# An attention and density kernel whose PSUM jobs no longer wait for the other bank's readers, with new caps on two engines' unused time

## The chip, the cores and the metric

The kernel runs on one core of a Trainium2 chip. The metric is the device time of one launch in microseconds; before the change the median of three runs is 4970.23 us (4967.25 to 4970.26). The profile is one further execution of the same program. TensorE (PE) does the matmuls and transposes, ScalarE (ACT) the activations, VectorE (DVE) reductions and elementwise work, GpSimd (POOL) some elementwise work, and SyncE (SP) issues the loads and stores.

## The reference

The input `x` is 8 images of 192 channels and 64 x 64 pixels, fp32. Two layers follow each other, each on a group norm of its input (32 groups) and each added to it.

```python
# layer 0: x = x + attention(_gn(x))
q = prelu(conv1x1(x, w1, b1), a1)            # 24 channels
k = prelu(conv1x1(x, w2, b2), a2)            # 24 channels
v = prelu(conv1x1(x, wa, ba), aa)            # 192 channels
score = jax.nn.softmax(jnp.einsum('bnc,bcm->bnm', q, k), axis=2)   # 4096 x 4096 per image
out = jnp.einsum('bnm,bmc->bnc', score, v)
# layer 1: x = x + density(_gn(x)); the chain below for x - 0.5 (lower) and for x + 0.5 (upper)
for i in range(4):                            # widths 1, 3, 3, 3, 1, weights per channel
    logits = jnp.einsum('cij,cjn->cin', softplus(ms[i]), logits) + bs[i]
    if i < 3:
        logits = logits + jnp.tanh(fs[i]) * jnp.tanh(logits)
sign = -jnp.sign(lower + upper)
likelihood = jnp.maximum(jnp.abs(sigmoid(sign * upper) - sigmoid(sign * lower)), 1e-6)
```

## The kernel before, in words

**Steps.** An image has 4096 queries in 8 blocks of 512, and a block is worked off in 16 steps of 256 keys, so an image takes 128 steps and the whole launch 1024. In step `t` the program writes, in this order: the score matmuls of the next step (`scores`, L738), the matmuls for a row maximum that will be needed 22 steps later (`max_products`, L669) and its reduce on VectorE (`max_reduce`, L677), the exponential on ScalarE (L742), and the eight products of the exponentials with the values (`attend`, L753), which accumulate in PSUM over a block's 16 steps. Then `work_off` adds everything else that falls into this step. The scores have one tile of two PSUM banks, the maxima have one, and two more such tiles (`turns`, named b0 and b1) take turns: one accumulates the block, the other is free for jobs. Each engine executes its own instructions in the order in which the program wrote them.

**Jobs.** A job is a piece of PSUM work that isn't part of the step: keys, queries and values of the next image (`keys`, L573; `queries`, L602; `values`, L630), the transposes that put the row maxima into the queries (`max_end`: `turn` L705, `add` L710), a block's output transposes (`finish`: `turn` L786, `residual` L795), the two small matmuls of a norm (`norm_end`: `mean` L420, `second`, `variance` L433, `third` L438) and the products that fold a norm into the weights (`weights`: `products`, `offsets`). `start_job` gives a job one bank or both of the free tile, and notes until which step it holds them. A job's matmuls come first; in the steps after that ScalarE or VectorE reads the result. Waits are derived from the order of accesses to a tile. A job in one bank therefore also waits for what earlier instructions read from the other bank of that tile.

**Density.** Layer 1 of an image is cut into 12 units (`Unit`, 128 x 1024 elements), and a unit into three lists of instructions, one for each of VectorE, ScalarE and TensorE. An image's units join the queue `units` when its second norm is known, which is some steps into the next image, and are worked off during that image's steps. VectorE's part is `scalar_tensor_tensor` (L995), ScalarE's are tanh (L963, L978) and scaled copies (L972, L988). In each step `density_step` adds a rate to each engine's credit. For VectorE the rate is found anew each step: the work left, spread over the steps up to a deadline of 10 steps past the next image, and a small addition. `Unit.step` then writes instructions while the credit is above zero, each costing about 1.2 us of it, and only those whose inputs were written in an earlier step. A job's cost is taken off as well. The credit is capped: VectorE's at twice the rate, ScalarE's at its own rate, which is 2.9 in the steps. Up to three units are worked at a time, the oldest first, and only the oldest is removed when its VectorE list is empty. The end of a pair of units (lower and upper) is `ending`: a few instructions on VectorE, ScalarE or GpSimd and a store.

**Ends of the launch.** Ahead of the steps stands a head that norms the first image and makes its keys, queries and values. After the last step comes a tail in which the last image's norm is found and its 12 units are worked off. There, 11 of the 12 units take their first mixing layer to TensorE (`product`, L936, in all four tiles; `gate1`, L954, follows on VectorE). In the tail the rate is 4.15 and the end of a pair stays on VectorE and ScalarE (`alone`).

Of the kernel before, what the change touches and what calls it, by code (L numbers as in the profile page):

```python
# [17 lines left out]
def kernel(  # L18
# [45 lines left out]
    F = 512  # L64
# [260 lines left out]


    homes = []

    scratch = []
    for k, cols in (("a", F), ("b", 2 * C)):  # L330
# [3 lines left out]
            pair.append(u)  # L334
        scratch.append(pair)
    ready = [0, 0]

    def start_job(t):
        p = t % STEPS
        for n, (rank, make, hold, banks, cols) in enumerate(jobs):  # L340
            if stream[0] and (p < 3 or p + max(hold, 1) >= STEPS):
                continue
            rooms = [(pm, g) for pm, g in homes if sum(k <= t for k in g) >= banks]
            if not rooms:
                if rank < 2:
                    return
                continue
            k = [i for i in (1, 0) if ready[i] <= t and scratch[i][0].shape[1] >= cols]
            if cols and not k:
                continue  # L350
            del jobs[n]
            pm, guest = min(rooms, key=lambda r: max(r[1]))
            at_ = [i for i in range(2) if guest[i] <= t]
            for i in at_[:banks]:
                guest[i] = t + hold + 1
            if cols:
                ready[k[0]] = t + 2
            parts = make(pm if banks == 2 else pm[:, at_[0], :], scratch[k[0]] if cols else None)
            for i, fn, cost, act, pe in parts:
                at(t + i, fn, cost, act, pe)  # L360
            return
# [47 lines left out]
    def norm_end(key, n, t, then=None):  # L409
# [7 lines left out]

        def mean():
            pm = cell["pm"]
            nc.tensor.matmul(pm[:, 0:2], lhsT=gavg, rhs=cell["mv"], start=True, stop=True)  # L420

        def second():
            mv, pm = cell["mv"], cell["pm"]
            res = cell["res"] = small.tile([128, 2], F32, tag="nrm", bufs=4, name=f"nrm_{nm}")
            nc.vector.tensor_copy(res, pm[:, 0:2])
            dv = cell["dv"] = small.tile([128, 2], F32, tag="dv", name=f"dv_{nm}")
            nc.vector.tensor_tensor(dv[:, 0:1], mv[:, 0:1], res[:, 0:1], ALU.subtract)
            nc.vector.tensor_tensor(dv[:, 0:1], dv[:, 0:1], dv[:, 0:1], ALU.mult)
            nc.vector.tensor_copy(dv[:, 1:2], dv[:, 0:1])

        def variance():
            pm = cell["pm"]
            nc.tensor.matmul(pm[:, 2:4], lhsT=gavg, rhs=cell["dv"], start=True, stop=True)  # L433

        def third():
            res, pm = cell["res"], cell["pm"]
            ve = cell["ve"] = small.tile([128, 1], F32, tag="ve", name=f"ve_{nm}")
            nc.vector.tensor_tensor(ve, res[:, 1:2], pm[:, 2:3], ALU.add)  # L438
# [36 lines left out]

        def make(pm, _):
            cell["pm"] = pm
            return [
                (0, mean, 0.0, 0.0, 0.4), (1, second, 0.8, 0.0, 0.0),
                (2, variance, 0.0, 0.0, 0.4), (3, third, 0.4, 0.0, 0.0),  # L480
            ]
# [7 lines left out]
    def weights(b, then):  # L489
        res = norms[b, 0]  # L490
        cell = {}

        def scale():
            for k, src, n in (("q", w1r, 2), ("k", w2r, 1), ("v", wa_sb, 1)):
                d = wf[k, b] = fold.tile(
                    [128, 3, src.shape[2]], F32, tag=f"w{k}", bufs=n, name=f"w{k}_{b}"
                )
                nc.scalar.activation(d, src, AF.Copy, scale=res[:, 1:2])
            mb = cell["mb"] = fold.tile([128, 128], F32, tag="mb", name=f"mb_{b}")
            nc.vector.tensor_copy(mb, res[:, 0:1].to_broadcast([128, 128]))  # L500

        def products():
            pf = cell["pf"]
            p = slice(0, R)
            for g in range(3):
                nc.tensor.matmul(
                    pf[:, 0:2], lhsT=wf["q", b][p, g, :], rhs=res[p, 0:2],
                    start=g == 0, stop=g == 2,
                )
            for g in range(3):  # L510
                nc.tensor.matmul(
                    pf[:, 2:4], lhsT=wf["k", b][:, g, :], rhs=res[:, 0:2],
                    start=g == 0, stop=g == 2,
                )
            for g in range(3):
                nc.tensor.matmul(
                    pf[:, 4 : 4 + C], lhsT=cell["mb"][p], rhs=wf["v", b][p, g, :],
                    start=g == 0, stop=g == 2,
                )

        def offsets():
            pf = cell["pf"]
            for k, src, at_, n in (("bq", bq, 0, 2), ("bk", bk, 2, 1)):
                d = wf[k, b] = fold.tile([128, 2], F32, tag=k, bufs=n, name=f"{k}_{b}")
                nc.vector.tensor_tensor(
                    d[:, 0:1], src[:, 0:1], pf[:, at_ : at_ + 1], ALU.subtract
                )
                nc.vector.tensor_scalar(d[:, 1:2], d[:, 0:1], -1.0, None, ALU.mult)
            d = wf["ba", b] = fold.tile([128, C], F32, tag="ba", name=f"ba_{b}")
            nc.vector.tensor_tensor(d, ba_row, pf[:, 4 : 4 + C], ALU.subtract)  # L530
            then()

        at(now[0] + 1, scale, 0.3, 2.0)
        def make(pf, _):
            cell["pf"] = pf
            return [(0, products, 0.0, 0.0, 2.0), (1, offsets, 1.0, 0.0, 0.0)]

        at(now[0] + 3, lambda: job(make, 1))
# [10 lines left out]

    made = set()  # L550

    def prelu(name, dst, src, bias, nslope, u):


        def first():
            for i, sign in enumerate((1.0, -1.0)):
                b_ = bias[:, i : i + 1] if bias is not None else 0.0
                nc.scalar.activation(u[i], src, AF.Relu, bias=b_, scale=sign)

        def last():  # L560
            nc.vector.scalar_tensor_tensor(dst, u[1], nslope, u[0], ALU.mult, ALU.add)
            made.add(name)

        return first, last

    def keys(b, d, what, done):
        t = xi[what, b, d]

        def make(pk, u):
            if b not in kt:  # L570
                kt[b] = kpool.tile([128, N // 4], F32, tag="k", name=f"k_{b}")
            for g in range(3):
                nc.tensor.matmul(  # L573
                    pk[:, 0:P], lhsT=wf["k", b][:, g, :], rhs=t[:, g, :],
                    start=g == 0, stop=g == 2,
                )
# [4 lines left out]
            first, last = prelu(  # L581
                ("k", b, d), kt[b][p, at_ : at_ + P], pk[p, 0:P], wf["bk", b][p], nslope[p, 1:2],
                [x[p, 0:P] for x in u],
            )
            return [
                (0, lambda: None, 0.0, 0.0, 1.3), (1, first, 0.0, 0.9, 0.0),
# [104 lines left out]
    def max_end(b, n):  # L691
# [10 lines left out]
        def turn():  # L702
            pt = cell["pt"]
            for t in range(4):
                nc.tensor.transpose(pt[:, t * 128 : (t + 1) * 128], nm[:, t, :], ident)  # L705

        def add():
            u = (n % 2) * 256
            q = qt[b, n // 2][:, :, u : u + 256]
            nc.vector.tensor_tensor(  # L710
                q, q, cell["pt"].rearrange("p (s t) -> p s t", s=2), ALU.add
            )
            made.add(("max", b, n))

        def make(pt, _):
            cell["pt"] = pt
            return [(0, turn, 0.0, 0.0, 0.8), (1, add, 0.7, 0.0, 0.0)]

        at(now[0], collect, 0.4)
# [140 lines left out]
    class Unit:  # L860
# [146 lines left out]
        def more(self, k):  # L1007
# [258 lines left out]
    for d in range(NP):  # L1266
# [1 line left out]
            norm_stat((0, 0), 2 * d + k, flat(xi["first", 0, d], k))  # L1268
    spread()
    negatives()  # L1270
    others = [
        ps_sc.tile([128, 2, F], F32, tag="sc", name="sc_head"),
        ps_mx.tile([128, 2, F], F32, tag="mx", name="mx_head"),
    ]
    homes.extend((t, [0, 0]) for t in turns + others)

    def go_on():
# [103 lines left out]
```

## Time and profile before

| what | value |
|---|---|
| median of three runs | 4970.23 us |
| the profiled execution's own time | 4970.59 us |
| its span, first to last instruction | 4968.6 us |
| PE busy in the span | 4785.8 us (96%) |
| DVE busy | 4301.2 us (87%) |
| ACT busy | 3202.4 us (64%) |
| POOL busy | 513.9 us (10%) |
| mean granted TensorE clock | 0.984 |

The profile's page shares out the span; a group line gives a source line, an engine, the tiles written and read, the count, the busy time and the mean of one, and what ended the idle time before them. A line of the waits view says who waited for whom: total us, times, longest. In a timeline row the start and the duration come first; brackets at its end tell how long the engine had been idle and what released it. PEld is the loading of weights, which overlaps the matmuls. A matmul in fp32 is recorded as two, so a step's eight `attend` products show as 16 rows. The steps fill the span from 93 to 4616 us, the head lies before, the tail behind.

### The profile page before, as it was taken

How to read it: one execution, taken by the hardware profiler on the slowest of the kernel's cores; microseconds unless marked ns; L12 is line 12 of the kernel's file. 1: busy time of each engine (PE TensorE's matmuls, PEld its weight loads, DVE VectorE, ACT ScalarE, POOL GpSimd, SP SyncE). 2: the span in 40 equal slices, each digit the busy share in tenths (PEclk: the TensorE clock that was granted, in tenths of full speed). 3: DMA queues.
4: the chain of work that ended last, by engine and by line, in shares of the span. 5: the costliest groups of instructions: out<-in, count | busy, mean ns of one | idle time of the engine just before them, and what ended most of it. 6: DMA issues, size and time to landing. Idle time of an engine off the chain costs nothing.

```text
span 4968.6 us, 69863 instructions
## 1 busy us (share of the span) xinstructions
PE 4785.8 (96%) x29152; PEld 3525.8 (71%) x29152; DVE 4301.2 (87%) x4442; ACT 3202.4 (64%) x3709; POOL 513.9 (10%) x506
## 2 busy tenths in 40 slices
PE   7999999999999999999999999999999999999596
PEld 5777777777777777777777777777777777777242
DVE  5433359999899989999899999999899999999888
ACT  2333346776667767777667766776677766776665
POOL 0000001111012110112011210110101110110000
PEclk9999999999999999999999999999999999999798
DMA  2000020011200111010200111011111111000000
GB/s 57 24 23 17 14 52 15 21 24 35 49 18 18 41 37 34 22 34 24 60 15 21 41 27 40 18 35 31 31 34 28 27 29 24 11 20 7 9 11 15
DMA packets 111953, 135.48 MB, mean 27 GB/s; under 512 B 14739, under 2 KB 93077, under 8 KB 111637
## 3 DMA queue, kind: packets, MB, share of 16 engines
q1 hardware_dynamic: 110432, 130.65, 10.9%
q8 instruction: 228, 3.74, 0.3%
q14 instruction: 89, 0.72, 0.1%
q10 hardware_dynamic: 1204, 0.37, 0.0%
HBM read 105.82 MB, written 25.17 MB: 26 GB/s over the span
## 4 chain that ended last, share of the span: by engine, by line
PE 73%; DVE 22%; ACT 3%; issue 1%; POOL 1%; DMA 0%; POOLq 0%; ACTq 0%; SPq 0%; DVEq 0%
PE b L753 43%; PE sc L738 17%; DVE d L995 14%; DVE rm L677 5%; PE b L630 3%; PE b L936 2%; PE b L602 1%; PE b L573 1%; PE mx L669 1%; PE sc_tail L936 1%; PE mx_tail L936 1%; PE b L786 1%; ACT d L988 1%; ACT d L963 1%; PE b L705 1%
## 5 line engine op out<-in xcount | busy, mean ns | idle before, releaser
L753 PEld LDWEIGHTS b<-v,e 128*128 128x128 f32 x16384 | 2668.4, 191 | 781.5 <-issue 781.5
L753 PE MATMUL b<-v,e 128*128 128x193 f32 x16384 | 2972.7, 335 | 0.0
L742 ACT ACTIVATE e<-sc 128x1024 f32<-128x1024 f32 x1024 | 1046.3, 1022 | 1422.6 <-PE mx L669 1373.3
L677 DVE TENSOR_REDUCE rm<-mx 128x1 f32<-128x1024 f32 x1002 | 1222.0, 1220 | 522.2 <-PE mx L669 518.5
L738 PE MATMUL sc<-q,k 25*128 25x512 f32 x4096 | 1159.7, 642 | 5.5 <-ACT e L742 5.2
L669 PE MATMUL mx<-k,q 24*128 24x512 f32 x4008 | 1135.6, 643 | 13.1 <-DVE rm L677 13.0
L995 DVE SCALAR_TENSOR_TENSOR d<-d,wsp,d 128x1024 f32<-128x1024 f32 x768 | 985.8, 1284 | 47.5 <-ACT d L988 35.4
L995 DVE SCALAR_TENSOR_TENSOR d<-d,lc,d 128x1024 f32<-128x1024 f32 x765 | 968.4, 1279 | 16.3 <-ACT d L972 3.3
L995 DVE SCALAR_TENSOR_TENSOR d<-d,tf,d 128x1024 f32<-128x1024 f32 x543 | 681.5, 1280 | 4.0 <-ACT d L978 3.9
L978 ACT ACTIVATE d<-d 128x1024 f32<-128x1024 f32 x543 | 570.1, 1055 | 70.8 <-DVE d L995 69.3
L738 PEld LDWEIGHTS sc<-q,k 25*128 25x128 f32 x4096 | 306.8, 183 | 238.6 <-issue 198.8
L1077 POOL MEMSET pause<- 128x1 f32 x240 | 23.7, 99 | 4007.4 <-DVE d L995 4007.4
L988 ACT ACTIVATE d<-d,cb,wsp 128x1024 f32<-128x1024 f32 x351 | 433.1, 1235 | 6.6 <-DVE d L995 5.3
L963 ACT ACTIVATE d<-xc,bn,wn 128x1024 f32<-128x1024 f32 x288 | 353.2, 1233 | 7.8 <-DVE bn L467 7.0
L669 PEld LDWEIGHTS mx<-k,q 24*128 24x128 f32 x4008 | 300.2, 183 | 40.1 <-DVE rm L677 39.9
L972 ACT ACTIVATE d<-xc,bn,wn 128x1024 f32<-128x1024 f32 x255 | 314.6, 1234 | 0.1
L1124 POOL TENSOR_TENSOR d<-d,d 128x512 f32<-128x512 f32 x80 | 167.9, 2098 | 0.1
L1112 POOL TENSOR_TENSOR d<-d,d 128x512 f32<-128x512 f32 x80 | 166.3, 2079 | 7.7 <-DVE d L995 7.1
L1132 POOL TENSOR_TENSOR d<-d,d 128x512 f32<-128x512 f32 x80 | 159.3, 1992 | 2.1 <-POOL pause L1077 0.3
L630 PE MATMUL b<-wv,xi 64*128 64x192 f32 x1344 | 139.5, 340 | 0.0
L630 PEld LDWEIGHTS b<-wv,xi 64*128 64x128 f32 x1344 | 106.5, 186 | 25.4 <-issue 23.8
L1116 ACT ACTIVATE d<-d 128x512 f32<-128x512 f32 x160 | 91.8, 623 | 32.1 <-POOL d L1112 26.0
(171 smaller groups left out, 2372.3 us busy)
## 6 DMA issues: line engine op xcount, KB each, us to landing
xi<-in_x_dram SPq DMA_DIRECT2D x392, 192.0 KB, 3.6
xc<-in_x_dram SPq DMA_DIRECT2D x64, 384.0 KB, 8.2
out_dram<-xc SPq DMA_DIRECT2D x96, 256.0 KB, 3.2
d<-in_x_dram SPq DMA_DIRECT2D x16, 192.0 KB, 4.3
d<-in_wat_dram ACTq DMA_DIRECT2D x2, 144.0 KB
cb<-in_den_b_dram SPq DMA_DIRECT2D x6, 2.2 KB, 2.1
ff<-in_den_f_dram SPq DMA_DIRECT2D x6, 2.2 KB, 2.1
bq<-in_b_dram ACTq DMA_DIRECT2D x4, 0.1 KB
```

The costliest lines, as they stand in the source:

```text
L630: nc.tensor.matmul(pv[:, s, 0:C], lhsT=t[p, g, k * 128 : k * 128 + 128] if g < 3 else one_row[p], rhs=wf["v", b][p, g, :] if g < 3 else wf ...
L669: nc.tensor.matmul(sc[:, s, :], lhsT=tile_of(qt[b, n // 2], n, j)[r], rhs=kt[b][r, u : u + F], start=True, stop=True,)
L677: nc.vector.tensor_reduce(out=rowmax[b, n][:, j, k : k + 1], in_=sc, axis=AX.XY, op=ALU.max)
L738: nc.tensor.matmul(sc[:, s, :], lhsT=kt[b][r, k : k + 128], rhs=qt[b, n // 2][r, :, u : u + 256], start=True, stop=True,)
L742: return lambda: nc.scalar.activation(e, sc, AF.Exp)
L753: nc.tensor.matmul(a[:, j, 0 : C + 1], lhsT=e[:, s, j * 128 : j * 128 + 128], rhs=v[:, s, p % 4, :], start=p == 0 and s == 0 and j % 2 == ...
L936: nc.tensor.matmul(out[:, h, :], lhsT=diag[g][:, 3 * i + n - 1 if n else 9 + i, :], rhs=src[:, h * F : h * F + F], start=n == 0, stop=n == 3,)
L963: nc.scalar.activation(self.buf[k], self.src(), AF.Tanh, bias=bn[:, s, g, 0, i : i + 1], scale=wn[:, g, 0, i : i + 1],)
L972: nc.scalar.activation(self.buf[k], self.src(), AF.Identity, bias=bn[:, s, g, 1, i : i + 1], scale=wn[:, g, 1, i : i + 1],)
L978: nc.scalar.activation(self.buf[k], self.buf["l", k[1], k[2]], AF.Tanh)
L988: nc.scalar.activation(self.buf[k], self.buf["l", n - 1, 0], AF.Identity, bias=offset, scale=wsp[:, g, w : w + 1],)
L995: nc.vector.scalar_tensor_tensor(dst, src, factor, dst, ALU.mult, ALU.add)
```

## The change

It has four parts. First, a job's matmuls (`write`) and the readers of its result (`read`) are registered so that a matmul in one bank is no longer ordered behind readers of the other bank of the same tile; this covers the norm's, the weights', the keys' and the maxima's jobs, those that hold one bank. Second, with two units left, the one with more VectorE work left goes first, a unit is removed as soon as its list is empty, and a pair's ending waits until both of its units are done. Third, in the steps the cap on the credits of VectorE and ScalarE becomes the rate plus 1.3; in the tail both caps stay as they were. Fourth, the deadline of an image's density is 15 steps past the next image instead of 10. The two tiles of the head are allocated earlier, so that they can be named.

```diff
+    def spotted():
+        n, i = spot[0]
+        def write(inst):
+            tc.declare_no_dep(inst.ins, group=f"turn{n}{1 - i}", reason="reads the other bank")
+        def read(inst):
+            tc.add_to_no_dep_group(f"turn{n}{i}", inst.ins)
+        return write, read
...
+            spot[0] = next(n for n, k in enumerate(turns + others) if k is pm), at_[0]
             parts = make(pm if banks == 2 else pm[:, at_[0], :], scratch[k[0]] if cols else None)
...
-            nc.tensor.matmul(pm[:, 0:2], lhsT=gavg, rhs=cell["mv"], start=True, stop=True)
+            cell["write"](
+                nc.tensor.matmul(pm[:, 0:2], lhsT=gavg, rhs=cell["mv"], start=True, stop=True)
+            )
...
-            nc.vector.tensor_tensor(ve, res[:, 1:2], pm[:, 2:3], ALU.add)
+            cell["read"](nc.vector.tensor_tensor(ve, res[:, 1:2], pm[:, 2:3], ALU.add))
...
         def make(pk, u):
...
+            write, read = spotted()
             for g in range(3):
-                nc.tensor.matmul(
+                write(nc.tensor.matmul(
                     pk[:, 0:P], lhsT=wf["k", b][:, g, :], rhs=t[:, g, :],
                     start=g == 0, stop=g == 2,
-                )
+                ))
...
-                nc.tensor.transpose(pt[:, t * 128 : (t + 1) * 128], nm[:, t, :], ident)
+                cell["write"](
+                    nc.tensor.transpose(pt[:, t * 128 : (t + 1) * 128], nm[:, t, :], ident)
+                )
...
                 b, c, g, s = self.key
-                if s == 1:
+                if not any(u.key == (b, c, g, 1 - s) and u.todo["DVE"] for u in units):
                     ending(b, c, g)
...
-            rate = left * COST["DVE"] / max(1, (units[0].key[0] + 2) * IMG + 10 - t) + OTHER
-        credit["DVE"] = min(credit["DVE"] + rate, 2 * rate)
+            rate = left * COST["DVE"] / max(1, (units[0].key[0] + 2) * IMG + 15 - t) + OTHER
         act = ACT_RATE if t < last else rate
-        credit["ACT"] = min(credit["ACT"] + act, act)
+
+        for eng, most in (("DVE", rate), ("ACT", act)):
+            more = (rate if eng == "DVE" else 0.0) if t >= last else 1.3
+            credit[eng] = min(credit[eng] + most, most + more)
         credit["PE"] = min(credit["PE"] + rate, rate)
         for eng in ("ACT", "PE", "DVE"):
-            for n in range(min(3, len(units))):
+            order = list(range(min(3, len(units))))
+            if len(units) == 2:
+
+                order.sort(key=lambda n: -len(units[n].todo["DVE"]))
+            for n in order:
                 units[n].step(eng, t, list(units)[:n])
-        while units and not units[0].todo["DVE"]:
-            units.popleft()
+        for u in [u for u in units if not u.todo["DVE"]]:
+            units.remove(u)
```

More of the change, by code (lines that the diff above doesn't have):

```diff
@@ L327 @@
     homes = []
+    others = [
+        ps_sc.tile([128, 2, F], F32, tag="sc", name="sc_head"),
+        ps_mx.tile([128, 2, F], F32, tag="mx", name="mx_head"),
+    ]
     scratch = []
@@ L336 @@
     ready = [0, 0]
+    spot = [None]
+    def spotted():
[5 more added lines that the diff above has]
+        return write, read
     def start_job(t):
@@ L424, in second @@
             res = cell["res"] = small.tile([128, 2], F32, tag="nrm", bufs=4, name=f"nrm_{nm}")
-            nc.vector.tensor_copy(res, pm[:, 0:2])
+            cell["read"](nc.vector.tensor_copy(res, pm[:, 0:2]))
             dv = cell["dv"] = small.tile([128, 2], F32, tag="dv", name=f"dv_{nm}")
@@ L432, in variance @@
             pm = cell["pm"]
-            nc.tensor.matmul(pm[:, 2:4], lhsT=gavg, rhs=cell["dv"], start=True, stop=True)
+            cell["write"](
+                nc.tensor.matmul(pm[:, 2:4], lhsT=gavg, rhs=cell["dv"], start=True, stop=True)
+            )
         def third():
@@ L477, in make @@
             cell["pm"] = pm
+            cell["write"], cell["read"] = spotted()
             return [
@@ L505, in products @@
             for g in range(3):
-                nc.tensor.matmul(
+                cell["write"](nc.tensor.matmul(
                     pf[:, 0:2], lhsT=wf["q", b][p, g, :], rhs=res[p, 0:2],
                     start=g == 0, stop=g == 2,
-                )
+                ))
             for g in range(3):
-                nc.tensor.matmul(
+                cell["write"](nc.tensor.matmul(
                     pf[:, 2:4], lhsT=wf["k", b][:, g, :], rhs=res[:, 0:2],
                     start=g == 0, stop=g == 2,
-                )
+                ))
             for g in range(3):
-                nc.tensor.matmul(
+                cell["write"](nc.tensor.matmul(
                     pf[:, 4 : 4 + C], lhsT=cell["mb"][p], rhs=wf["v", b][p, g, :],
                     start=g == 0, stop=g == 2,
-                )
+                ))
         def offsets():
@@ L524, in offsets @@
                 d = wf[k, b] = fold.tile([128, 2], F32, tag=k, bufs=n, name=f"{k}_{b}")
-                nc.vector.tensor_tensor(
+                cell["read"](nc.vector.tensor_tensor(
                     d[:, 0:1], src[:, 0:1], pf[:, at_ : at_ + 1], ALU.subtract
-                )
+                ))
                 nc.vector.tensor_scalar(d[:, 1:2], d[:, 0:1], -1.0, None, ALU.mult)
             d = wf["ba", b] = fold.tile([128, C], F32, tag="ba", name=f"ba_{b}")
-            nc.vector.tensor_tensor(d, ba_row, pf[:, 4 : 4 + C], ALU.subtract)
+            cell["read"](nc.vector.tensor_tensor(d, ba_row, pf[:, 4 : 4 + C], ALU.subtract))
             then()
@@ L535, in make @@
             cell["pf"] = pf
+            cell["write"], cell["read"] = spotted()
             return [(0, products, 0.0, 0.0, 2.0), (1, offsets, 1.0, 0.0, 0.0)]
@@ L550, with prelu @@
     made = set()
-    def prelu(name, dst, src, bias, nslope, u):
+    def prelu(name, dst, src, bias, nslope, u, read=lambda inst: None):
         def first():
@@ L557, in first @@
                 b_ = bias[:, i : i + 1] if bias is not None else 0.0
-                nc.scalar.activation(u[i], src, AF.Relu, bias=b_, scale=sign)
+                read(nc.scalar.activation(u[i], src, AF.Relu, bias=b_, scale=sign))
         def last():
@@ L571, in make @@
                 kt[b] = kpool.tile([128, N // 4], F32, tag="k", name=f"k_{b}")
+            write, read = spotted()
             for g in range(3):
-                nc.tensor.matmul(
+                write(nc.tensor.matmul(
                     pk[:, 0:P], lhsT=wf["k", b][:, g, :], rhs=t[:, g, :],
                     start=g == 0, stop=g == 2,
-                )
+                ))
             done()
@@ L582, in make @@
                 ("k", b, d), kt[b][p, at_ : at_ + P], pk[p, 0:P], wf["bk", b][p], nslope[p, 1:2],
-                [x[p, 0:P] for x in u],
+                [x[p, 0:P] for x in u], read,
             )
@@ L704, in turn @@
             for t in range(4):
-                nc.tensor.transpose(pt[:, t * 128 : (t + 1) * 128], nm[:, t, :], ident)
+                cell["write"](
+                    nc.tensor.transpose(pt[:, t * 128 : (t + 1) * 128], nm[:, t, :], ident)
+                )
         def add():
@@ L709, in add @@
             q = qt[b, n // 2][:, :, u : u + 256]
-            nc.vector.tensor_tensor(
+            cell["read"](nc.vector.tensor_tensor(
                 q, q, cell["pt"].rearrange("p (s t) -> p s t", s=2), ALU.add
-            )
+            ))
             made.add(("max", b, n))
@@ L716, in make @@
             cell["pt"] = pt
+            cell["write"], cell["read"] = spotted()
             return [(0, turn, 0.0, 0.0, 0.8), (1, add, 0.7, 0.0, 0.0)]
@@ L1270 @@
     negatives()
[L1271 to L1274, printed above, removed]
     homes.extend((t, [0, 0]) for t in turns + others)
```

## The prediction

> **What bounds the kernel now.** I read the page's busy shares first, then a stretch of the middle by windows, then TensorE's waits up to the end of the attention steps, then the timeline around two of the waits, and last the windows of the end.
>
> ```profile
> PE 4785.8 (96%) x29152; PEld 3525.8 (71%) x29152; DVE 4301.2 (87%) x4442; ACT 3202.4 (64%) x3709; POOL 513.9 (10%) x506
> ...
> 1800.00:2400.00 600.00, 593.24 (x3753) 446.93 (x3755) 570.60 (x583) 415.91 (x484) 76.74 (x72) 0.99 0.13 31
> ```
>
> The second line is a stretch of the middle: wall time, then PE, PEld, DVE, ACT and POOL, the granted clock, the DMA share. TensorE is busy for 593 of 600 us and VectorE for 571. Both are nearly full, so what counts is where one waits for the other. A quiet step takes 3.88 us (L738 starts at 2456.77 and again at 2460.65), and 1024 steps run from 93 to 4616. "Busy" hides short waits, because a matmul is drawn 0.33 us long but starts every 0.16. So I count from start to start: 3.88 us, plus 1.5 us for values or queries, 1.3 keys, 0.65 output transposes, 0.44 maxima transposes, 0.12 each norm product and 2.7 weight products. That makes 4399 us, and what the steps take beyond it is 126 us: 2 in the first image and 14 to 20 in each later one. 31 of the 126 is the clock: its record has fourteen half-speed stretches of 3.41 us and two of 6.83 between 93 and 4616, 61 us, half of it lost. The other 95 us is waiting, and TensorE's waits up to 4615 us name the visible part:
>
> ```profile
> PE mx L669 <- DVE rm L677: 13.0, 18, 1.5
> PE b L573 <- DVE q L710: 12.0, 12, 2.7
> PE b L705 <- DVE ve L438: 11.6, 5, 2.3
> PE sc L738 <- ACT e L742: 5.2, 10, 2.3
> PE b L705 <- ACT prb L558: 2.1, 5, 0.4
> ```
>
> Lines two and three are jobs that wait for a reader of the other bank of their tile. Here is one of each kind, a bank wait and a VectorE burst:
>
> ```profile
> 1840.73 2.48 DVE L995 SCALAR_TENSOR_TENSOR d<-d,tf,d 128x1024 f32<-128x1024 f32 x2
> ...
> 1843.12 1.22 DVE L677 TENSOR_REDUCE rm<-mx 128x1 f32<-128x1024 f32 x1
> ...
> 1844.72 0.14 DVE L438 TENSOR_TENSOR ve<-nrm,b 128x1 f32<-128x1 f32 x1
> ...
> 1844.91 0.66 PE L705 MATMUL b<-ident,negmax 128*128 128x128 f32 x4 [2.32 <-DVE ve L438]
> ```
>
> ```profile
> 1871.14 6.29 DVE L995 SCALAR_TENSOR_TENSOR d<-d,lc,d 128x1024 f32<-128x1024 f32 x5
> ...
> 1878.62 1.13 PE L669 MATMUL mx<-k,q 24*128 24x512 f32 x4 [1.51 <-DVE rm L677]
> ...
> 1879.67 4.56 PE L753 MATMUL b<-v,e 128*128 128x193 f32 x16
> ```
>
> In the first, four transposes stand behind a one-column reader of the other bank, which itself stands behind a reduce that two density instructions made late. In the second, five density instructions hold back the reduce and so the next maxima. The last row is that step's attend at 4.56 us, where 2.88 is usual: the clock was halved.
>
> After the steps comes the last image:
>
> ```profile
> 4618.40:4657.50 39.10, 2.71 (x10) 2.14 (x10) 35.49 (x40) 23.05 (x44) 0.00 (x0) 0.53 0.05 13
> ...
> 4933.50:4968.60 35.10, 0.00 (x0) 0.00 (x0) 22.45 (x19) 11.97 (x11) 0.00 (x0) 0.57 0.12 30
> ```
>
> In the first row TensorE has no work until the norm is known, and VectorE, through which that chain runs in order, is busy for 35.5 of 39.1 us. The second row is the end after the last product.
>
> **The change, part by part.** The instructions are the same in number and kind; only waits and order change. Durations are those between issues (L995 1.20 us, L677 1.14, the exponential 0.92).
>
> *Bank waits.* In the changed program's order the maxima transposes wait for `third` 0 times (7 before) and for `residual` 0 times (5 before), `keys` for `add` 7 times (21), and for ScalarE's PReLU readers 27 times (34). The output transposes wait for `add` 10 times (1) and for `third` no longer (5). The 29 waits of maxima transposes for PReLU readers, the 2.1 us row, stay. The rows at stake are 11.6 + 12.0 = 23.6 us. Not all comes back. At 1843 the next maxima would still wait for the reduce, which ends at 1844.34, so of 2.32 us about 1.1 would only move there. From start to start this step loses 2.55 us, of which 0.9 belongs to the burst; the five such waits give 5 x 1.64 = 8 here, the keys up to 12. I take 16 us, with 0 (all moves to the reduce) and 24 as ends. Five attends newly wait for `offsets` of the weights; these end at 2504.3, in the step after their products, long before the next attend that opens a bank. Zero, and about 1.5 us each without that cover.
>
> *VectorE's cap.* An image has 12 x 23 density instructions; 276 x 1.22 over some 138 steps, plus 0.1, is a rate of 2.5 us. The cap was twice that, about 5.1, and becomes 3.8. Between two reduces the old order has five density instructions 13 times and four 55 times, the new order 0 and 39. The reduce starts 1.24 us into a step and takes 1.14, so VectorE may be 1.4 us late, plus the step's jobs, before TensorE notices. A step of five: 1.14 + 0.55 + 0.17 + 5 x 1.20 = 7.9 us against 5.3, so 2.6, and that is what the step at 1876 lost besides the clock. Going through the steps in order, carrying the lateness along and taking off what was already waited, the old order gives 51 us of the 95, the new one 12. Gain 39 us, ends 30 and 45.
>
> *ScalarE's cap.* From 2.9 to 4.2, so 42 steps hold four density activations where none did: 0.92 + 4 x 1.1 = 5.3 us, 1.45 over a quiet step. The exponential usually ends 1.7 us before the next scores need it, which hides one such step; followed by jobs it doesn't. The same summing gives 0 before and 7 us after. VectorE may then wait for a late tanh: today its waits for ScalarE in the middle come to 8 us (3.9 + 3.6 + 0.5). I add 4, with 0 and 15 as ends. Cost 11.
>
> *The clock.* Each short half-speed stretch costs 1.7 us. Of 18 windows (two stretches are double), twelve follow a wait for `ve` (4), a burst of five (7) or keys that waited (1, at 849); five, at 781, 1354, 2501 and 3648, follow the weight products, small matmuls that stay, and one is at the start. The Trainium skill's TensorE: Matmul & The Clock Gate (the table under "Why this matters for your kernels") asks only for no idle gaps over about 3 us. By that rule waits of 1.5 and 2.3 us would not throttle and this term is 0 and the forecast 4939. The row above halves the clock right after 1.5, so I go by the row: 9 of the 12 windows, 15 us, ends 0 and 20.
>
> *The later deadline.* Density is spread to 15 steps past the next image instead of 10. For the last spread this leaves work behind: between the last `invert` and the last norm VectorE's order has 37 full-size instructions where it had 26. With the small ones the sum is 49.3 us instead of 36.1, and VectorE runs in order with only 3.6 us idle there. So the norm, and all of TensorE's products behind it, come 10 to 14 us later; I take 12. ScalarE's evacuations stand some 4 us later in its queue, hidden by the 15 VectorE instructions ahead of `residual`.
>
> *The last two units.* They change only the end. After the last product's gate the new order has 18 VectorE instructions, the old one 15. The three extra, 3.7 us, fit into gaps of 2.25 and 2.31 that end in adds waiting for ScalarE; the first pair comes 1.5 us later for it. The last gate comes about 1 us earlier: it now waits from 4934.64 to 4936.12 for VectorE's queue. Zero, ends -2 and +3.
>
> *Queues.* SyncE's order of loads and stores moves with the density. TensorE waits for no load in the steps, and a load lands 3.6 us after its issue, at least four steps (15.5 us) ahead of use. GpSimd's order is the same. Zero; without that cover, a few us at one load of an image.
>
> Sum: -16 - 39 + 11 - 15 + 12 = -47. From the profiled execution's 4970.6 (span 4968.6 and 2.0 around it, 0.4 above the median) that gives **4924 us**.
>
> **Rivals.** (a) *The bank waits only move.* VectorE at 95% is the real limit, the clock stretches stay: -39 + 11 + 12 = -16, 4955 us. For it: the reduce at 1844.34. Against it: of the 12 keys waits most show no late reduce beside them. (b) *More comes back.* All of the 95 us of waits but 20, and 20 of the clock, less 12 at the end: -83, 4888. For it: the smoother order may also relieve waits that my sums leave unexplained (95 - 51 - 20 = 24). Against it: nothing in the change aims at them. (c) *Slower: ScalarE's bursts.* A fourth activation makes the exponential and VectorE's next operand late, and each of the 42 steps costs its whole 1.45 us: 61. With no gain in the clock, -16 - 39 + 61 + 12 = +18, 4989. The gain of 55 less 12 is used up at 43 / 1.45 = 30 of the 42 steps. Against it: 1.7 us of slack and ScalarE at 69% there. (d) *Nothing measurable:* (a) with part of (c), ten steps of it, 4969.
>
> **How the numbers follow.** Likeliest 0.50 (its own range 4904 to 4943), (a) 0.20, (b) 0.18, (c) 0.06, (d) 0.06. A measurement of this kernel can tell 0.2%, about 10 us, from no change. Faster: 0.50 + 0.18 + most of (a) = 0.85; same: (d) and the slow edge of (a) = 0.08; slower: 0.07. The range 4880 to 4960 leaves out (c), (d) and the far ends of (a) and (b).
>
> **What would show it.** Right: no wait of L705 for `ve`, the keys' waits for `add` down to a third, no row of five L995, the half-speed windows in the steps down from 18 to about 9, the steps ending near 4557 instead of 4616; the gap to the last norm at 50 us or more, the end after the last product still near 35. Wrong: the maxima's wait for the reduce grown by what the jobs' waits lost, half-speed stretches as before, or waits of the scores for the exponential well over 10 us.

## The result, and the profile after

The changed kernel takes 4918.36 us (median of four runs, 4916.79 to 4920.2), and the kernel before 4970.24 us beside it: a ratio of 0.9895, 95% interval 0.9878 to 0.9913. The forecast was 4924. The profiled execution's span fell from 4968.6 to 4915.0 us.

The page's busy shares and a stretch of the middle, of the changed kernel (columns as before):

```profile
PE 4740.1 (96%) x29152; PEld 3505.3 (71%) x29152; DVE 4312.6 (88%) x4442; ACT 3194.5 (65%) x3709; POOL 514.0 (10%) x506
...
1800.00:2400.00 600.00, 596.47 (x3800) 451.69 (x3799) 580.80 (x608) 423.76 (x490) 74.96 (x72) 1.00 0.14 34
```

VectorE is now busy for 581 of 600 us in the middle (571 before). TensorE's waits between 640 and 4540 us, from the second image's steps to the last, are three rows:

```profile
PE sc L769 <- ACT e L773: 14.2, 20, 1.6
PE mx L697 <- DVE rm L705: 4.9, 7, 0.8
PE b L658 <- ACT pra L585: 1.4, 1, 1.4
```

In the changed kernel's line numbers L769 is the scores, L697 the maxima, L705 the reduce (in the kernel before, L705 was the transposes), L734 the transposes, L773 the exponential and L658 the values.

The rows for `ve` and for the keys behind `add` are gone, the maxima's wait for the reduce is down from 13.0 to 4.9 us, and the scores' wait for the exponential has grown: over all the steps it is 16.4 us where it was 5.2. The place that stood for the bank waits looks like this now, in the timeline:

```profile
1822.15 0.14 DVE L462 TENSOR_TENSOR ve<-nrm,b 128x1 f32<-128x1 f32 x1
...
1822.40 2.60 DVE L1026 SCALAR_TENSOR_TENSOR d<-d,wsp,d 128x1024 f32<-128x1024 f32 x2
...
1822.71 0.60 PE L734 MATMUL b<-ident,negmax 128*128 128x128 f32 x4
...
1823.24 0.70 PE L769 MATMUL sc<-q,k 25*128 25x512 f32 x2
```

Here `ve` is done before the transposes; that they no longer wait for it is seen in the run with the bank waits alone. Where the time went is best seen in three stretches: the norm's chain between the last `invert` (the reciprocal at the end of a block) and the last norm, then TensorE's products, then what is left after the last product.

```profile
4552.00:4603.50 51.50, 2.71 (x10) 2.14 (x10) 49.62 (x58) 33.09 (x54) 0.00 (x0) 0.55 0.04 10
4603.50:4878.60 275.10, 237.60 (x528) 102.05 (x528) 227.89 (x200) 184.26 (x177) 0.00 (x0) 0.95 0.04 10
4878.60:4915.00 36.40, 0.03 (x1) 0.00 (x0) 25.98 (x22) 14.06 (x13) 0.00 (x0) 0.54 0.11 29
```

The first is 51.5 us, with VectorE busy for 49.6 of it. Counted in the same way, to ScalarE's first diagonal (L871, the weights of the products that use the norm), it was 40.4 before:

```profile
4618.40:4658.80 40.40, 2.71 (x10) 2.14 (x10) 36.62 (x48) 23.09 (x45) 0.00 (x0) 0.53 0.05 13
```

The second is the same (274.6 before); the third is 36.4 (35.2).

All runs are split up in the same way below. "Steps" runs from the first scores of the first step to those of the last. "Waits" is what is left of it after 4393 us for 1023 undisturbed steps with their jobs and after half of the time at half clock. "Windows" counts the half-speed windows of 3.41 us in the steps, "end" is everything behind the steps. "Maxima" is largely part of the waits. In a quiet step the first matmul of the maxima starts 0.013 us after the first one of the scores; the column adds up how much later it starts. Wherever that is more than 0.05 us, in all these runs, a reduce on VectorE had ended 0.05 to 0.06 us before: it is the lateness of VectorE, as TensorE feels it. The row of the waits view shows less of it (13.0 of 59.5 us before), since it counts only time in which no matmul is drawn. These five columns come from the profiled execution of each run.

| kernel | median us | ratio to before, interval | steps | waits | maxima | windows | end |
|---|---|---|---|---|---|---|---|
| before | 4970.24 | | 4518.8 | 95.5 | 59.5 | 18 | 356.8 |
| changed | 4918.36 | 0.9895 (0.9878 to 0.9913) | 4451.3 | 48.5 | 29.0 | 6 | 369.6 |
| bank waits alone | 4952.72 | 0.9968 (0.9955 to 0.9981) | 4499.7 | 83.2 | 69.0 | 14 | 357.6 |
| both caps alone | 4946.33 | 0.9956 (0.9939 to 0.9972) | 4493.1 | 80.0 | 35.7 | 12 | 358.0 |
| units in turn alone | 4951.81 | 0.9968 (0.9956 to 0.9980) | 4499.8 | 78.2 | 32.7 | 17 | 356.9 |
| deadline 15 alone | 4996.24 | 1.0057 (1.0042 to 1.0072) | 4539.3 | 104.1 | 84.4 | 25 | 362.9 |
| VectorE's cap alone | 4948.88 | 0.9961 (0.9946 to 0.9975) | 4495.0 | 88.7 | 53.6 | 8 | 360.1 |
| ScalarE's cap alone | 4957.25 | 0.9977 (0.9968 to 0.9986) | 4503.2 | 83.3 | 37.8 | 16 | 358.6 |
| changed, deadline 10 | 4920.65 | 0.9903 (0.9888 to 0.9918) | 4466.3 | 61.7 | 45.7 | 7 | 357.7 |
| changed, VectorE's old cap | 4922.40 | 0.9909 (0.9894 to 0.9924) | 4460.6 | 54.4 | 37.3 | 8 | 369.6 |
| changed, ScalarE's old cap | 4917.41 | 0.9899 (0.9885 to 0.9914) | 4454.6 | 53.5 | 45.6 | 5 | 367.0 |
| changed, last deadline 0 | 4908.96 | 0.9884 (0.9867 to 0.9900) | 4480.4 | 77.6 | 56.2 | 6 | 333.3 |
| changed, deadlines 13 and 0 | 4909.19 | 0.9881 (0.9866 to 0.9896) | 4476.5 | 61.7 | 31.4 | 13 | 336.8 |
| changed, held until the norm | 4910.05 | 0.9885 (0.9868 to 0.9901) | 4451.1 | 48.3 | 29.0 | 6 | 363.3 |

The ratios are to runs of the kernel before on the same chip in the same comparison (medians 4964.6 to 4970.2). One program's executions differ in the windows: the kernel before ran in 4963.7 to 4974.0 us, the slower ones at a granted clock of 0.984 instead of 0.985. If the clock is all of it, that is six windows (an estimate, at half of 3.41 us each), so a difference of a few windows between two rows can be chance. The column of the maxima is steadier: the changed kernel and the one held until the norm, whose steps are the same, both have 29.0. From before to changed the steps lost 67.5 us: 47.0 of waits and 20.5 of half clock. The end took 12.8 longer, and the head 1.1, which leaves the 53.6 us by which the span fell.

### The profile page after: what moved, and what is told of

Same layout as the page of the kernel before. It is cut to its first block, busy times and chain, and to the rows that moved or that the text cites. A ratio compares the mean times of both kernels' runs of the same rounds, so it can differ in the third digit from the quotient of the medians.

```text
span 4915.0 us, 69887 instructions
## 1 busy us (share of the span) xinstructions
PE 4740.1 (96%) x29152; PEld 3505.3 (71%) x29152; DVE 4312.6 (88%) x4442; ACT 3194.5 (65%) x3709; POOL 514.0 (10%) x506
## 4 chain that ended last, share of the span: by engine, by line
PE 78%; DVE 16%; ACT 4%; issue 1%; POOL 1%; DMA 0%; ACTq 0%; SPq 0%; DVEq 0%; POOLq 0%
PE b L784 46%; PE sc L769 18%; DVE d L1026 10%; DVE rm L705 4%; PE b L658 4%; PE b L967 2%; PE b L630 2%; PE b L601 1%; PE sc_tail L967 1%; PE mx_tail L967 1%; PE mx L697 1%; PE b L817 1%; ACT d L1019 1%; ACT d L1009 1%; ACT e L773 1%
## 5 line engine op out<-in xcount | busy, mean ns | idle before, releaser
L773 ACT ACTIVATE e<-sc 128x1024 f32<-128x1024 f32 x1024 | 1046.7, 1022 | 1456.3 <-PE mx L697 1414.0
L705 DVE TENSOR_REDUCE rm<-mx 128x1 f32<-128x1024 f32 x1002 | 1223.3, 1221 | 459.6 <-PE mx L697 454.2
L769 PE MATMUL sc<-q,k 25*128 25x512 f32 x4096 | 1155.2, 640 | 16.8 <-ACT e L773 16.4
L697 PE MATMUL mx<-k,q 24*128 24x512 f32 x4008 | 1130.4, 640 | 4.9 <-DVE rm L705 4.9
L1026 DVE SCALAR_TENSOR_TENSOR d<-d,lc,d 128x1024 f32<-128x1024 f32 x765 | 981.6, 1291 | 18.1 <-ACT d L1003 5.1
L769 PEld LDWEIGHTS sc<-q,k 25*128 25x128 f32 x4096 | 306.2, 182 | 250.2 <-issue 195.8
L994 ACT ACTIVATE d<-xc,bn,wn 128x1024 f32<-128x1024 f32 x288 | 354.1, 1236 | 2.8 <-DVE bn L491 2.0
L697 PEld LDWEIGHTS mx<-k,q 24*128 24x128 f32 x4008 | 299.6, 182 | 16.9 <-DVE rm L705 13.5
L658 PE MATMUL b<-wv,xi 64*128 64x192 f32 x1344 | 139.5, 340 | 1.4 <-ACT pra L585 1.4
L658 PEld LDWEIGHTS b<-wv,xi 64*128 64x128 f32 x1344 | 106.5, 186 | 26.9 <-issue 20.9
L967 PE MATMUL b<-d,v 128*128 128x512 f32 x204 | 95.2, 618 | 17.0 <-ACT d L994 17.0
```

Source lines behind the costliest of these rows:

```text
L658: nc.tensor.matmul(pv[:, s, 0:C], lhsT=t[p, g, k * 128 : k * 128 + 128] if g < 3 else one_row[p], rhs=wf["v", b][p, g, :] if g < 3 else wf ...
L697: nc.tensor.matmul(sc[:, s, :], lhsT=tile_of(qt[b, n // 2], n, j)[r], rhs=kt[b][r, u : u + F], start=True, stop=True,)
L705: nc.vector.tensor_reduce(out=rowmax[b, n][:, j, k : k + 1], in_=sc, axis=AX.XY, op=ALU.max)
L769: nc.tensor.matmul(sc[:, s, :], lhsT=kt[b][r, k : k + 128], rhs=qt[b, n // 2][r, :, u : u + 256], start=True, stop=True,)
L773: return lambda: nc.scalar.activation(e, sc, AF.Exp)
L967: nc.tensor.matmul(out[:, h, :], lhsT=diag[g][:, 3 * i + n - 1 if n else 9 + i, :], rhs=src[:, h * F : h * F + F], start=n == 0, stop=n == 3,)
```

## The experiments

**Bank waits alone.** The kernel before with the registering of writes and reads; caps, deadline and order as before.

```diff
             spot[0] = next(n for n, k in enumerate(turns + others) if k is pm), at_[0]
...
-                nc.tensor.matmul(
+                write(nc.tensor.matmul(
```

> The kernel before with the bank waits alone taken away; caps, deadline and order of units as before. The prediction's terms: -16 us for the waits and about -6 of its -15 for the clock (five of its twelve windows follow such waits), so 4948 us. Rival (a), the waits only move to the reduce: no wait of L705 for ve left, but the maxima's wait for the reduce grown from 13 us by about as much, and 4965 to 4975 us.

Measured: 4952.72 us, 17 less. TensorE's waits between 640 and 4580 us:

```profile
PE mx L697 <- DVE rm L705: 14.6, 23, 1.5
PE sc L769 <- ACT e L773: 9.1, 13, 0.9
PE b L734 <- ACT prb L585: 2.1, 5, 0.4
```

The rows of 11.6 and 12.0 us are gone. In the same window of the kernel before, the reduce's row was 13.0, and the exponential's was

```profile
PE sc L738 <- ACT e L742: 3.0, 9, 1.0
```

The place that stands at 1840 to 1845 us in the kernel before shows what became of a bank wait:

```profile
1834.91 0.60 PE L734 MATMUL b<-ident,negmax 128*128 128x128 f32 x4
...
1835.44 1.13 PE L769 MATMUL sc<-q,k 25*128 25x512 f32 x4
...
1836.88 1.13 PE L697 MATMUL mx<-k,q 24*128 24x512 f32 x4 [0.31 <-DVE rm L705]
1837.21 0.14 DVE L462 TENSOR_TENSOR ve<-nrm,b 128x1 f32<-128x1 f32 x1
```

The transposes start 2.3 us before `ve` (0.2 us after it in the kernel before), but the maxima start 1.44 us behind the scores, because the reduce is still late; the row shows 0.31 of that. Over the steps the maxima are 9.5 us later than before (69.0 instead of 59.5), and the exponential's row has grown by 6.1. All waits together fell by 12.3 us: of the 23.6 us about half moved and half stayed away. The windows fell from 18 to 14, 6.8 us, within what executions of one program differ by. Rival (a), that all of it moves, falls: 17 us are gone.

**Both caps alone.** The kernel before with the new caps, deadline 10.

```diff
-        credit["DVE"] = min(credit["DVE"] + rate, 2 * rate)
-        credit["ACT"] = min(credit["ACT"] + act, act)
+        for eng, most in (("DVE", rate), ("ACT", act)):
+            more = (rate if eng == "DVE" else 0.0) if t >= last else 1.3
+            credit[eng] = min(credit[eng] + most, most + more)
```

> The kernel before with both caps at the rate plus 1.3 and nothing else changed (deadline 10). Here no step has five density instructions, 56 have four, and 47 have four activations. The summing of the prediction gives waits of 27 us instead of 51, plus 4 for VectorE behind ScalarE, and 7 clock windows at stake, of which some 9 us come back: about 4941 us. The rival that ScalarE's bursts cost their whole 1.45 us each: 47 x 1.45 = 68, less 29 and 9: 5000 us.

Measured: 4946.33 us, 24 less, near the forecast of the sums. The bursts of ScalarE, 47 steps of them, are no loss as a whole: the maxima start 23.8 us less late, and the scores' wait for the exponential (640 to 4580 us) is 13.3 us instead of 3.0. Rival (c) falls.

**Units in turn alone.** The kernel before with the order of the last two units, their removal and the ending's condition changed.

```diff
-            for n in range(min(3, len(units))):
+            order = list(range(min(3, len(units))))
+            if len(units) == 2:
+                order.sort(key=lambda n: -len(units[n].todo["DVE"]))
+            for n in order:
                 units[n].step(eng, t, list(units)[:n])
-        while units and not units[0].todo["DVE"]:
-            units.popleft()
+        for u in [u for u in units if not u.todo["DVE"]]:
+            units.remove(u)
```

> The kernel before with the last two units in turn alone. The prediction costed this at nothing, acting at the end alone: 4968 to 4973 us. The rival: two units are also left at the end of every image's density, and there the order spreads the work; summing VectorE's work per step gives 35 us of waits instead of 51, so 4954 us.

Measured: 4951.81 us, 18 less, all of it in the steps; the end is the same (356.9 us). The prediction's "they change only the end" is wrong. Two units are also left at the end of every image's density. VectorE's order first departs from the old one at about 1190 us, near the end of the second image's steps. Over all the steps it has four density instructions between two reduces 38 times instead of 55, and five 14 times instead of 13. The waits view shows what such a part does to its neighbours (640 to 4580 us):

```profile
PE b L573 <- DVE q L710: 24.1, 12, 2.7
PE b L705 <- DVE ve L438: 12.2, 5, 2.5
PE mx L669 <- DVE rm L677: 7.9, 8, 1.0
```

The reduce's row fell from 13.0 to 7.9 us, while the keys' bank waits doubled from 12.0 to 24.1. These rows together don't fall; the gain is in what they leave out, the start of the maxima, 32.7 us late in all instead of 59.5. With the bank waits taken away as well, nothing of those 24 us is left.

**The changed kernel with deadline 10.**

```diff
-            rate = left * COST["DVE"] / max(1, (units[0].key[0] + 2) * IMG + 15 - t) + OTHER
+            rate = left * COST["DVE"] / max(1, (units[0].key[0] + 2) * IMG + 10 - t) + OTHER
```

> The changed kernel with the deadline back at 10 steps. If the later deadline only leaves work behind at the end, as the prediction has it: 12 us less, 4906 us, the stretch between the last invert and the last norm back from about 52 to 40 us. If it is the later deadline that keeps the steps smooth, the steps lose more than 12 us and the time is 4920 us or more; the sums of work per step give 7 us more there, 4913.

Measured: 4920.65 us. The end is 11.9 us shorter, as expected, with the norm's stretch at 39.3 us; but the steps are 15.0 us longer, with the maxima 45.7 us late instead of 29.0. The later deadline pays for itself in the steps and is worth 2 us in the runs, less than they can tell.

**Deadline 15 alone,** in the kernel before: the reverse of that edit's line.

```diff
-            rate = left * COST["DVE"] / max(1, (units[0].key[0] + 2) * IMG + 10 - t) + OTHER
+            rate = left * COST["DVE"] / max(1, (units[0].key[0] + 2) * IMG + 15 - t) + OTHER
```

> The kernel before with deadline 15 alone. VectorE's order has 30 full-size instructions in the end stretch instead of 26 (5 us more). If a later deadline smooths the steps by itself, as it does in the changed kernel (15 us): 4960 us. If it does so only together with the other parts, the sums per step (80 us instead of 51, 22 steps of five density instructions instead of 13) hold: about 5000 us.

Measured: 4996.24 us, slower by 0.57% (0.42 to 0.72). TensorE's waits between 640 and 4600 us begin with

```profile
PE mx L669 <- DVE rm L677: 37.7, 20, 4.7
PE sc L738 <- ACT e L742: 8.5, 10, 1.1
PE b L573 <- DVE q L710: 6.0, 16, 0.6
```

37.7 us behind the reduce instead of 13.0, and 25 half-speed windows instead of 18. The rows for `ve` are gone here with no bank wait taken away: they depend on where VectorE's other work falls. The same line that gives the changed kernel 15 us in its steps costs the kernel before 20. A deadline only sets the rate; in the kernel before it gave 22 steps of five density instructions instead of 13, in the changed kernel there is none. Which of the other parts makes that difference was not run. The sums of work per step had told the sign and the size (about 5000).

**VectorE's cap alone.**

```diff
-        credit["DVE"] = min(credit["DVE"] + rate, 2 * rate)
+        credit["DVE"] = min(credit["DVE"] + rate, rate + (rate if t >= last else 1.3))
```

> The kernel before with VectorE's cap alone. No step has five density instructions, 60 have four; the sums per step give 32 us of waits instead of 51, and the seven clock windows that follow a burst of five are at stake: 19 and up to 12 us, so 4940 to 4950 us. If the cap gives what the prediction put down to it (39 us and 9 for the clock): 4922.

Measured: 4948.88 us, 0.39% less. The steps lost 23.8 us, of which 17 are ten half-speed windows and only 6.8 are waits; the maxima are 53.6 us late instead of 59.5. The time lies in the range expected, but 19 us of waits and 12 of the clock had been expected. The prediction had put 39 us of waits down to this cap.

**VectorE's cap undone** in the changed kernel.

```diff
-            more = (rate if eng == "DVE" else 0.0) if t >= last else 1.3
+            more = (rate if eng == "DVE" else 0.0) if t >= last else 1.3 if eng == "ACT" else rate
```

> The changed kernel with VectorE's cap back at twice the rate. If the cap is what brings the gain from VectorE's bursts, as the prediction put it, the time goes back by 39 us, to 4957. Rival: with the units in turn, the later deadline and ScalarE's cap the work rarely piles up so far that the cap matters (three steps of five instead of none; the sum of waits is 21.5 us instead of 19): 4918 to 4923 us.

Measured: 4922.40 us, 4 more than the changed kernel by the medians, 7 by the ratios, with intervals that overlap; the steps are 9.3 us longer, and the maxima 37.3 us late instead of 29.0. Alone the cap is worth 0.39%, on top of the other parts 0.08 to 0.14%. The parts cure the same bursts: with the old cap there are three steps of five density instructions here, and 13 in the kernel before.

**ScalarE's cap alone.**

```diff
-        credit["ACT"] = min(credit["ACT"] + act, act)
+        credit["ACT"] = min(credit["ACT"] + act, act + (0.0 if t >= last else 1.3))
```

> The kernel before with ScalarE's cap alone, 52 steps with four density activations. If it only costs, as the prediction has it, 4981 us and the scores' wait for the exponential at 16 us instead of 5. If it also lets VectorE work more evenly (six steps of five density instructions instead of 13, 39 of four instead of 55; sums 33 and 11 us instead of 51 and 0): 4955 to 4965 us.

Measured: 4957.25 us, a gain. Three rows of the waits (640 to 4580 us):

```profile
PE sc L738 <- ACT e L742: 20.9, 22, 2.1
...
PE mx L669 <- DVE rm L677: 9.9, 8, 1.5
...
PE b L573 <- DVE q L710: 1.0, 2, 0.7
```

The exponential's row grew from 3.0 to 20.9 us, and the reduce's fell from 13.0 to 9.9, the keys' from 12.0 to 1.0. By these rows alone nothing is gained. The gain is again in the start of the maxima, 37.8 us late instead of 59.5. VectorE has five density instructions between two reduces 6 times instead of 13, and four 39 times instead of 55, as the second branch of the expectation had it.

**ScalarE's cap undone** in the changed kernel.

```diff
-            more = (rate if eng == "DVE" else 0.0) if t >= last else 1.3
+            more = (rate if eng == "DVE" else 0.0) if t >= last else 1.3 if eng == "DVE" else 0.0
```

> The changed kernel with ScalarE's cap back at its rate (no step with four activations any more). By the prediction's term for it, which is a cost of 11 us, 4907 us, and the scores' wait for the exponential back from 16.4 us to about 5. Rival: the bursts also bring VectorE's operands in time; without them the sum of VectorE's lateness is 21 us instead of 12, which uses up most of it: 4915 to 4920 us.

Measured: 4917.41 us, the same as the changed kernel. The scores' wait for the exponential (640 to 4540 us) is back at

```profile
PE sc L769 <- ACT e L773: 6.2, 10, 1.1
```

from 14.2, so the cap does cost these 8 us. Yet all waits together are 53.5 us, not less than the 48.5 with the cap, because the maxima are then 45.6 us late instead of 29.0.

**Deadline 0 for the last spread** in the changed kernel.

```diff
-            rate = left * COST["DVE"] / max(1, (units[0].key[0] + 2) * IMG + 15 - t) + OTHER
+            rate = left * COST["DVE"] / max(1, (units[0].key[0] + 2) * IMG + (15 if units[0].key[0] < B - 2 else 0) - t) + OTHER
```

> The changed kernel with deadline 0 for the last spread alone, so that the last but one image's density ends with the steps. VectorE's order has 4 full-size instructions between the last invert and the last norm instead of 37 (9.6 us in sum, not 49.3), so that stretch should fall from 51.5 us to some 15 to 20. If the sums per step hold, the last image's steps pay 27 us for it: 4910 us. If VectorE does the added work in time that it has unused in the last image: 4884 us. The prediction's claim that this stretch is set by VectorE's order falls if it stays above 40 us.

Measured: 4908.96 us. The windows of the norm's stretch and of the last image's steps:

```profile
4580.20:4595.40 15.20, 2.05 (x10) 1.64 (x10) 9.73 (x25) 13.66 (x37) 0.00 (x0) 0.60 0.14 35
4028.80:4573.60 544.80, 538.73 (x3122) 395.31 (x3122) 530.12 (x500) 395.80 (x430) 91.11 (x81) 1.00 0.07 16
```

The stretch fell from 51.5 to 15.2 us: it is VectorE's order that sets it. The last image's steps took 544.8 instead of 515.6 us, 29 more (the sums said 27), because VectorE is then busy for 530 of them; the maxima are 27 us later in sum. Of the 36 us won at the end 7 are left. With the two that follow, from which the runs can't tell it apart, this is the fastest kernel of the study: 8 us under the run with ScalarE's old cap in the same comparison, 9 us under the changed kernel's median of another.

**Deadlines 13 and 0.** As that, with 13 for the other images.

```diff
-            rate = left * COST["DVE"] / max(1, (units[0].key[0] + 2) * IMG + 15 - t) + OTHER
+            rate = left * COST["DVE"] / max(1, (units[0].key[0] + 2) * IMG + (13 if units[0].key[0] < B - 2 else 0) - t) + OTHER
```

> As the run before, and deadline 13 instead of 15 for the other images. The sums per step give 29 us of waits for the steps instead of the changed kernel's 19, and the end is 32 to 37 us shorter: about 4893 us. If the sums don't tell 13 from 15 apart in truth, the same time as the run before.

Measured: 4909.19 us, the same as with 15 and 0. The waits are 15.9 us fewer, as the sums said, but there are seven more half-speed windows, 12 us, which the sums don't know. The expected 4893 us did not come.

**Held until the norm.** In the changed kernel no density is written between the last step and the last norm.

```diff
     def density_step(t, rate):
+        if t >= last and (B - 1, 1) not in norms:
+            return
```

> The changed kernel (deadline 15), but after the last step no density is written until the last norm is known. The steps keep all their gain, unlike in the run with deadline 0, and the stretch between the last invert and the last norm falls from 51.5 to about 15 us. The work held back, some 46 us of VectorE, comes behind the norm, where VectorE is idle for 40 of the 262 us of the products. If it fits there, the stretch of the products grows by 10 us or less: 4892 us. If VectorE is the limit there too, the time is given back and it is 4910 or more.

Measured: 4910.05 us. The norm's stretch is 16.2 us, the products' stretch 304.1 instead of 275.1. The window of that stretch, and the first row of TensorE's waits from 4540 us on:

```profile
4566.30:4870.40 304.10, 233.56 (x528) 100.38 (x528) 269.37 (x235) 204.33 (x195) 0.00 (x0) 0.90 0.04 9
```

```profile
PE b L967 <- ACT d L994: 59.4, 6, 52.0
```

The second row is one wait of 52 us: the first product that needs a tanh of `xc` (L994) stands until ScalarE has written it. In ScalarE's order that tanh is the 29th activation behind the diagonals, and most of those ahead of it belong to the held-back older units; in the changed kernel it is the seventh. The stretch of that wait:

```profile
4568.80:4622.57 53.77, 1.77 (x3) 0.23 (x2) 53.10 (x45) 33.84 (x32) 0.00 (x0) 0.50 0.00 0
```

ScalarE is busy for 34 of these 54 us and waits for VectorE for 19; VectorE is busy for 53. So VectorE is the limit here, as the second branch of the expectation had it, though over the whole 304 us it is busy for only 269. What was moved behind the norm still stood in front of TensorE, by the rule that the oldest unit goes first. Whether another order of the units would keep these 29 us was not tried.

## Why the prediction was right

The size came from the right sums, but several of them carried the wrong name, and the split between them was off. What the units in turn, and the bank waits, are worth on top of the other parts was not run.

*Bank waits, -16.* Measured alone: 12.3 us of waits and 6.8 of clock. Right in size, and right that part of the visible 23.6 us moves (about 11 did).

*VectorE's cap, -39.* This step failed. The sum itself, 51 us of lateness falling to 12, was made over the changed program's order, which is the work of all four parts; the prediction booked it on the cap. Measured, the maxima's lateness falls from 59.5 to 29.0 us with all parts and to 53.6 with the cap alone. The cap alone takes 6.8 us of waits and 17 of clock, and undoing it costs 4 to 7 us. Waits also fall by 17.3 us with the units in turn alone and, in company with the other parts, by 13.2 with the later deadline. The whole forecast for waits, -16 - 39 + 11 = -44, met -47, with luck in the split: the maxima gave 30.5 instead of 39, and the rows for `ve` and the keys all of their 23.6 instead of 16.

*ScalarE's cap, +11.* The cost is there: the scores' wait for the exponential grew by 11.2 us, where the sum had 7; the other 4, VectorE behind a late tanh, did not come (9.0 us of such waits in the middle, 8 before). That the cap is a net cost is wrong. Undone, it changes nothing, since the maxima give back 16.6 us where the scores gain 8, and alone it gains 0.23%. "Well over 10 us" of the scores' wait was named as a sign of a wrong forecast; 16.4 came, beside the time forecast. That sign was badly chosen, since the forecast itself put 7 us on top of 5.2.

*The clock, -15.* Twelve of 18 windows went, 20.5 us, where nine were expected (counts from one execution each, so twelve and nine can't be told apart). No wait of TensorE in the steps of the kernel before was longer than 2.7 us, and the windows named for `ve` (1846, 2419, 2993, 3566) are gone when only the bank waits are. Here the rule of the Trainium skill's TensorE: Matmul & The Clock Gate, no idle gaps over about 3 us, is too lenient, and the row was the better guide. With the rule the forecast would have been 4939. Five of the six windows left in the changed kernel (222, 1349, 1912, 3038, 3601) follow the weight products, as expected; the sixth (1284) follows a wait for the reduce.

*The later deadline, +12.* Right at the end of the changed kernel (12.8 us, the norm's stretch 11.1 longer by VectorE's order); in the kernel before the same deadline adds 6.1 there. The prediction left out what the deadline does in the steps: 15 us gained there.

*The last two units, 0.* Right after the last product (36.4 us instead of 35.2) and wrong in the steps, where it put them at nothing and they give 19.0 us alone. The failed sentence is "they change only the end".

*Queues, 0.* No row of TensorE's waits in the steps names a load, before or after.

Of the rivals, (a) and (c) fell by the runs with the bank waits and the caps alone; (b) asked for 4888, and 48.5 us of waits remain instead of 20; (d) asked for 4969.

## What to carry to other kernels

When two engines are both nearly full, add up each engine's work per step in program order and carry the lateness along: those sums told the size of the whole change, the loss by the deadline alone, and the price of moving work into the last image (27 us said, 29 paid). Don't book such a sum on one edit. Edits of a planner that cure the same bursts overlap (VectorE's cap: 0.39% alone, about 0.1% on top of the rest) or lose their cost in company (the deadline: 0.57% slower alone, no loss with the rest). Measure lateness from start to start: the idle time in a row of waits showed 13.0 of 59.5 us. And look at what a planner leaves behind at its last turn: a serial chain through an engine that works in order costs all that was queued ahead of it. Finishing that work earlier and holding it back both took 35 us off the chain here, and both paid four fifths of it back elsewhere.

## What the runs showed of the hardware that was not expected

The half-speed windows can weigh as much as the waits they follow. In the kernel with VectorE's cap alone ten windows fewer brought 17 us while the waits fell by 6.8; with deadlines 13 and 0 seven more took back 12 of 16 us. All four runs of each bear it out in the granted clock: 0.987 with the cap alone and 0.984 to 0.985 before; 0.987 with deadlines 13 and 0 and 0.989 to 0.991 with 15 and 0. Nearly all windows in the steps of these runs come right after a wait of TensorE, from 0.4 us (VectorE's cap alone, at 2468) to 3.3 us of drawn idle time (deadline 15 alone), or after the small weight products, at which no idle time is drawn: 12 matmul records of two columns and 6 of 192. Not every such wait or product has one. After the weight products of seven images there are windows four times in the kernel before, five times in the changed one, and never in the kernel with the units in turn alone.

The program alone doesn't set them. The changed kernel and the one held until the norm give TensorE, VectorE and ScalarE the same instructions in the same order up to the last step, and each has six windows: at 222, 1284, 1349, 1912, 3038 and 3601 us in the one, at 97, 779, 1346 (two), 2476 and 3039 in the other. What decides it in a given case was not settled here.
